# Role adapters: first projections by eight samples of one role, on two Strassen levels, with the weights stationary

## The chip, the core and the metric

The kernel runs on one core of one Trainium2 chip. Its time is device microseconds from launch to end, the median of several runs on the chip. One execution is also recorded by the hardware profiler; its trace gives the durations used here. PE is the matrix engine (PEld its weight loads), DVE the vector engine, ACT the scalar engine, POOL GpSimd, SP the engine whose queue issues nearly all DMAs. SBUF is the on-chip memory of 128 partitions, PSUM the matrix engine's accumulators in banks of 512 f32 columns, DRAM the chip's main memory.

## What is computed

128 samples, each a 128 x 1024 f32 matrix, go through two layers. In each layer a sample uses the weights of its own role, which is in an input list; there are three sets of weights.

```python
for W_down, b_down, W_up, b_up, gamma, beta in layers:     # two layers
    h = gelu(x @ W_down[role] + b_down[role])              # 1024 -> 512, per sample
    y = x + h @ W_up[role] + b_up[role]                    # 512 -> 1024
    x = layernorm(y) * gamma[role] + beta[role]
```

All of it is in f32.

## The kernel before

**Order of the samples.** A short sort on the chip, mostly on DVE, counts the roles and puts the samples into slots, so that slots 2n and 2n+1 hold two samples of one role: 63 such pairs, and a last item of two samples whose roles may differ. `perm` gives the sample of a slot, `place` its role's place; both are read into registers (`reg`).

**Four phases.** Layer 0 down, layer 0 up, layer 1 down, layer 1 up, each over 64 items. A down item reads two samples (`quartered`, L399: four DMAs of 128 KB each per sample), transposes them on DVE (`turn`, L557), multiplies by `W_down`, applies the Gelu and stores the hidden states to a DRAM buffer `hd`. An up item reads `hd`, transposes it (L668 to L671), multiplies by `W_up`, adds the sample, normalises and stores the result to a DRAM buffer `mid` or to the output.

**Strassen on a pair.** The two samples of a pair are the two row blocks of the left matrix; its columns are halved, and the weights are cut into four blocks. Winograd's form of Strassen's method needs seven products of blocks where the plain way needs eight. The left sums (`winograd_sums`, L413) are four operations on POOL. The right sums, T1 to T4, are made once for each role (`Sums`, L173): loaded into the room of the tables, summed on DVE, stored to DRAM (`scratch`), and loaded from there for the phase. SBUF holds the seven blocks of all three roles (`wall`), and a product picks its role by a register in the address. In `product` (L423) the samples are the stationary operand and the weights the moving one, 256 columns in a down phase, 512 in an up phase:

```python
nc.tensor.matmul(ps[:, 0:cols], a[:, j], w.rhs(r, j, cols), ...)
```

The products of an item accumulate in PSUM banks of three groups, `b` (3 banks), `e` (3) and `a` (2). ACT first copies the bias into a bank (`seeded`). Between products DVE or ACT copies partial results out of a bank (`begin`, `end`, `whole`; called evictions here), and a later product adds to the same bank. The last item has the two samples alone, four products each.

**Order of the work.** `at(time, step)` puts a step into a heap; at the end the steps are issued in order of time, and each engine executes its instructions in that order. The unit is one product of a pair, four matmuls of 256 columns or two of 512; an item takes seven units, and its seven products stand two units apart, so that two items' products alternate on PE. `Down.PREPARE`, `Up.PREPARE` and the loop at L865 set how far ahead loads, transposes and sums stand. All DMAs of this loop stand in SP's queue, in the same order of time, and wait there for the buffers that they fill or read.

The first item of layer 0 is different (`plain`, L589): its two samples belong to the commonest role and are multiplied without Strassen, since their weights have only just arrived.

Of the kernel before, what the change touches and what calls it, by code (L numbers as in the profile page):

```python
# [11 lines left out]
I32 = mybir.dt.int32  # L12
AF = mybir.ActivationFunctionType
# [6 lines left out]
P = 128  # L20
# [6 lines left out]
def kernel(  # L27
# [11 lines left out]

# [4 lines left out]
    NPAIR = (B - R + 1) // 2  # L61
    NFIRST = -(-B // R) // 2
    W = H
    ORDER = ["B11", "B21", "T2", "T1", "T3", "B22", "T4"]

    const = ctx.enter_context(tc.tile_pool(name="const", bufs=1))
    wpool = ctx.enter_context(tc.tile_pool(name="weights", bufs=1))
    work = ctx.enter_context(tc.tile_pool(name="work", bufs=2))
# [3 lines left out]

    NI = NPAIR + 1
    hd = [dram.tile([2, S * K], F32, tag=f"hd{n}", name=f"hd{n}") for n in range(NI)]
    mid = [dram.tile([2, S, H], F32, tag=f"mid{n}", name=f"mid{n}") for n in range(NI)]
    scratch = {
        (layer, up): {
            t: dram.tile([P, R, W], F32, tag=f"{t}_{layer}{up}", name=f"{t}_{layer}{up}")
            for t in ORDER
        }  # L80
        for layer in range(2)
        for up in (0, 1)
    }

    def flat(tag, bufs, name, size=2048):
        return work.tile([P, size], F32, tag=tag, name=name, bufs=bufs)


    NSLOT = 8
    wall = wpool.tile([P, NSLOT, R * W], F32, name="wall")  # L90

    class Block:


        def __init__(self, slot):
            self.slot = slot
            self.v = wall[:, slot].rearrange("p (r n) -> p r n", n=W)

        def rhs(self, r, j, cols):
            return self.v[:, ds(r, 1), ts(j, cols)]  # L100

    class Half:


        def __init__(self, v, half):
            self.v, self.half = v, half

        def rhs(self, r, j, cols):
            return self.v[:, ds(r, 1), j, self.half]

    tables = wpool.tile([P, 3, R * H], F32, name="tables")

    def table(v, which):
        n = v.shape[1]
        t = tables[:, which].rearrange("p (r n) -> p r n", r=R)[:, :, 0:n]

        def load(places=range(R), queue=nc.sync):
            for k in places:  # L120
                r = reg(role_of, k, [queue.engine], R - 1)
                queue.dma_start(t[:, k], v[ds(r, 1), :].to_broadcast((P, n)))

        return t, load

    def bias_table(v, which):

        n = v.shape[1] // 2
        t, load = table(v, which)

        def subtract(places=slice(0, R)):
            right, left = t[:, places, n:], t[:, places, 0:n]
            nc.vector.tensor_tensor(right, right, left, ALU.subtract)

        return t, load, subtract


    rows_of = [
        wall[:, 2 * k : 2 * k + 2]
        .rearrange("p k n -> p (k n)")  # L140
        .rearrange("p (r j h c) -> p r j h c", r=R, h=2, c=K // 2)
        for k in range(2)
    ]

    def load_rows(k, place, queue):
        role = reg(role_of, place, [queue.engine], R - 1) if place else reg(role_0, 0, [queue.engine], R - 1)
        src = layers[0][0][ds(role, 1)].rearrange("o (p m) c -> p (o m) c", p=P)
        queue.dma_start(rows_of[k][:, place].rearrange("p j h c -> p j (h c)"), src[:, ts(k, NQ)])

    first_weights = {  # L150
        "B11": Half(rows_of[0], 0),
        "B21": Half(rows_of[1], 0),
        "B22": Half(rows_of[1], 1),
        "T3": Half(rows_of[0], 1),
        "T1": Block(4),
        "T2": Block(5),
        "T4": Block(6),
    }

    def first_sum(name, place):  # L160
        b11, b12, b21, b22 = (rows_of[k][:, :, :, h] for k in range(2) for h in range(2))
        t1, t2, t4 = (
            first_weights[n].v.rearrange("p r (j c) -> p r j c", c=K // 2) for n in ("T1", "T2", "T4")
        )
        o, a, b = {
            "T1": (t1, b12, b11),
            "T2": (t2, b22, t1),
            "T3": (b12, b22, b12),
            "T4": (t4, b21, t2),
        }[name]  # L170
        nc.vector.tensor_tensor(o[:, place], a[:, place], b[:, place], ALU.subtract)

    class Sums:  # L173

        def __init__(self, layer, up, k):
            self.w = layers[layer][2 if up else 0]
            self.rows = "o (m i) c -> i (o m) c" if up else "o (i m) c -> i (o m) c"
            self.k = k  # L180
            n = self.w.shape[2] // 2
            room = tables[:, 0:2].rearrange("p t n -> p (t n)")
            self.whole = room[:, 0 : 4 * W].rearrange("p (m c) -> p m c", c=2 * n)
            block = lambda t: t.rearrange("p (j c) -> p j c", c=n)
            quarter = room[:, 0 : 4 * W].rearrange("p (k j h c) -> p k h j c", k=2, h=2, c=n)
            self.at = {
                "B11": quarter[:, 0, 0],
                "B12": quarter[:, 0, 1],
                "B21": quarter[:, 1, 0],
                "B22": quarter[:, 1, 1],  # L190
                "T1": block(room[:, 4 * W : 5 * W]),
                "T2": block(room[:, 5 * W : 6 * W]),
            }
            self.at["T3"], self.at["T4"] = self.at["B12"], self.at["B21"]
            self.to = {name: block(t[:, k]) for name, t in scratch[layer, up].items()}

        def load(self, q):
            if q == 0:
                self.role = reg(role_of, self.k, [ENG.SP], R - 1)
            rows = self.w.shape[1] // NQ  # L200
            src = self.w[ds(self.role, 1), ds(q * rows, rows), :]
            nc.sync.dma_start(self.whole[ts(q, SQ)], src.rearrange(self.rows, i=SQ))

        def sum(self, name):
            a, b = {"T1": ("B12", "B11"), "T2": ("B22", "T1"), "T3": ("B22", "B12"), "T4": ("B21", "T2")}[name]
            nc.vector.tensor_tensor(self.at[name], self.at[a], self.at[b], ALU.subtract)

        def store(self, name):
            nc.sync.dma_start(self.to[name], self.at[name])

    class Phase:
        def __init__(self, layer, up):
            self.layer, self.up, self.weights = layer, up, {}
            self.vectors = layers[layer][3:] if up else layers[layer][1:2]
            if up:
                self.gamma, self.load_gamma = table(self.vectors[1], 1)
                self.beta, self.load_beta = table(self.vectors[2], 2)

        def new_bias(self, which):
            self.next_bias, self.load_bias, self.subtract = bias_table(self.vectors[0], which)  # L220

# [827 lines left out]
```

## Time and profile before

| what | us |
|---|---|
| median of 3 runs (3123.8 to 3123.97) | 3123.83 |
| profiled execution | 3123.5 span, nothing outside it counted |
| PE busy | 3111.5 |
| DVE, POOL, ACT busy | 1975.9, 1770.7, 1200.7 |
| DVE busy in 200 us of a down phase of layer 0 / of an up phase | 100.0 / 155.7 |
| POOL busy in the same | 91.5 / 140.6 |
| products of the first item end | 31.9 |
| last product of an up item in layer 1 begins | 3110.9 |

The profile has one line for a group of instructions: source line, engine, operation, the tile written and the tiles read, shapes and count; then the busy time and the mean duration of one; then the time that the engine was idle just before them and what ended it. Matmuls are pipelined, so that the durations of neighbours overlap; their true spacing is read from the chain or from starts. The chain of waits follows the work that ended last back to the start. A matmul of f32 operands appears as two instructions.

### The profile page before, as it was taken

To read this page: it belongs to the slowest core of one execution; us is meant where nothing else is said; L and a number is where in the kernel's file an instruction comes from. 1 tells how busy PE (TensorE), PEld (TensorE's weight loads), DVE (VectorE), ACT (ScalarE), POOL (GpSimd) and SP (SyncE) were. 2 spreads that over 40 slices of the span, in tenths; PEclk is the share of its full clock that TensorE was granted. 3 is DMA by queue.
4 is the path that set the end of the run, shared out by engine and by line. 5 is a ranking of instruction groups with operands and counts; after the bars stand their busy time and mean duration, and the time that the engine had idled before them with its cause. 6 is when DMAs were issued, how large, how long until landed. Compare 5 with 4: busy or idle time off the path is not lost.

```text
span 3123.5 us, 42240 instructions
## 1 busy us (share of the span) xinstructions
PE 3111.5 (100%) x10796; PEld 2048.3 (66%) x10796; DVE 1975.9 (63%) x2814; ACT 1200.7 (38%) x2813; POOL 1770.7 (57%) x1388
## 2 busy tenths in 40 slices
PE   9999999999999999999999999999999999999999
PEld 6888888888544444444488888888884444444443
DVE  6554544544678777777864444444447877777777
ACT  1222222222454545555432222222224545554544
POOL 3544344444577767777654443434436777677775
PEclk9999999999999999999999999999999999999999
DMA  8778788886786565666687555555567765656564
GB/s 218 197 216 209 209 207 210 213 209 194 272 293 236 215 223 215 218 220 217 230 237 182 144 128 135 126 130 134 128 189 272 282 235 210 226 204 230 208 230 174
DMA packets 429880, 642.22 MB, mean 206 GB/s; under 512 B 35794, under 2 KB 305875, under 8 KB 428500
## 3 DMA queue, kind: packets, MB, share of 16 engines
q1 hardware_dynamic: 429074, 637.15, 66.4%
q8 instruction: 102, 1.67, 0.2%
q10 hardware_dynamic: 578, 2.36, 0.2%
q14 instruction: 126, 1.03, 0.1%
HBM read 405.02 MB, written 234.36 MB: 205 GB/s over the span
## 4 chain that ended last, share of the span: by engine, by line
PE 50%; DVE 0%; issue 0%; ACT 0%; DVEq 0%
PE bu L427 14%; PE bd L427 14%; PE eu L427 7%; PE ed L427 7%; PE au L427 4%; PE ad L427 3%; DVE ou L725 0%; DVE last_stat L701 0%; DVE xu L700 0%; ACT ou L809 0%; DVEq L1045 0%; DVE xu L694 0%; DVE last_mv L719 0%; DVEq L365 0%; ACT meanu L807 0%
## 5 line engine op out<-in xcount | busy, mean ns | idle before, releaser
L427 PE MATMUL bu<-wall,hTu 128*128 (+1 forms) x2048 | 921.4, 592 | 0.4 <-DVE xu L694 0.4
L558 DVE STREAM_TRANSPOSE xTd<-xqd 128x1024 f32<-128x1024 f32 (+1 forms) x252 | 504.5, 2065 | 348.5 <-PE bd L427 280.8
L427 PEld LDWEIGHTS bu<-wall,hTu 128*128 128x128 f32 x2048 | 389.0, 190 | 488.1 <-issue 454.4
L418 POOL TENSOR_TENSOR Sd<-xTd 128x512 f32<-128x512 f32 x123 | 158.5, 1289 | 791.1 <-DVE xTd L558 787.6
L811 POOL TENSOR_TENSOR varu<-varu,mhalf 128x1 f32<-128x1 f32 x254 | 327.2, 1288 | 394.6 <-ACT varu L810 394.6
L427 PE MATMUL eu<-wall,hTu 128*128 (+1 forms) x1040 | 488.0, 592 | 0.0
L427 PE MATMUL bd<-wall,xTd 128*128 (+1 forms) x2048 | 483.1, 379 | 0.0
L427 PE MATMUL bd<-wall,Sd 128*128 (+1 forms) x2000 | 472.5, 379 | 0.0
L427 PEld LDWEIGHTS bd<-wall,xTd 128*128 128x128 f32 x2048 | 389.1, 190 | 54.2 <-issue 1.4
L427 PEld LDWEIGHTS bd<-wall,Sd 128*128 128x128 f32 x2000 | 380.0, 190 | 52.9 <-issue 1.4
L818 DVE SCALAR_TENSOR_TENSOR ou<-xu,meanu,tables 128x1024 f32<-128x1024 f32 x253 | 325.9, 1288 | 134.3 <-ACT ou L809 120.1
L624 ACT ACTIVATE hd<-hd 128x256 f32<-128x256 f32 x379 | 157.8, 417 | 531.3 <-DVE hd L623 531.3
L427 PEld LDWEIGHTS eu<-wall,hTu 128*128 128x128 f32 x1040 | 197.6, 190 | 247.5 <-issue 219.1
L805 ACT ACTIVATE partu<-statu 128x2 f32<-128x2 f32 x254 | 51.6, 203 | 729.6 <-DVE xu L703 729.6
L809 ACT ACTIVATE ou<-xu,meanu 128x1024 f32<-128x1024 f32 x254 | 291.7, 1148 | 8.6
L826 POOL TENSOR_TENSOR ou<-ou,tables 128x1024 f32<-128x1024 f32 x123 | 290.1, 2359 | 0.0
L694 DVE TENSOR_TENSOR xu<-bu,xu 128x512 f32<-128x512 f32 x256 | 176.0, 687 | 118.3 <-PE bu L427 118.3
L427 PE MATMUL ed<-wall,xTd 128*128 (+1 forms) x1056 | 249.1, 379 | 0.0
L418 POOL TENSOR_TENSOR hTu<-hTu 128x256 f32<-128x256 f32 x126 | 198.1, 1573 | 70.7 <-DVE hTu L669 47.5
L427 PE MATMUL au<-wall,hTu 128*128 (+1 forms) x504 | 236.8, 592 | 0.0
L427 PE MATMUL ed<-wall,Sd 128*128 (+1 forms) x1000 | 236.2, 379 | 0.0
L427 PE MATMUL ad<-wall,xTd 128*128 (+1 forms) x992 | 234.3, 379 | 0.0
(146 smaller groups left out, 3395.8 us busy)
## 6 DMA issues: line engine op xcount, KB each, us to landing
xqd<-in_x_dram SPq DMA_DIRECT2D x512, 128.0 KB, 3.2
hd<-hd SPq DMA_DIRECT2D x256, 256.0 KB, 2.4
xu<-in_x_dram SPq DMA_DIRECT2D x128, 512.0 KB, 3.8
mid<-ou SPq DMA_DIRECT2D x128, 512.0 KB, 4.4
xu<-mid SPq DMA_DIRECT2D x128, 512.0 KB, 3.8
out_dram<-ou SPq DMA_DIRECT2D x125, 512.0 KB, 3.7
hqu<-hd SPq DMA_DIRECT2D x244, 256.0 KB, 5.0
xqd<-mid SPq DMA_DIRECT2D x488, 128.0 KB, 3.8
```

The lines of the kernel that those rows point to most:

```text
L418: engine.tensor_tensor(dst[:, 1], a11, a21, ALU.subtract)
L427: nc.tensor.matmul(ps[:, 0:cols], a[:, j], w.rhs(r, j, cols), start=start and j == 0, stop=j == n - 1, skip_group_check=True,)
L558: nc.vector.transpose(self.a[:, s, chunks].rearrange("p j (t a) -> p j a t", t=SQ), self.xq[s].rearrange("p a (i j) -> p j a i", i=SQ)[:, ...
L624: nc.scalar.activation(y, y, AF.Gelu)
L694: nc.vector.tensor_tensor(y, ps, y, ALU.add)
L805: nc.scalar.mul(part, self.stat[:, s], -1.0 / H)
L809: nc.scalar.activation(box["o"], self.x[:, s], AF.Square, bias=m, accum_out=v)
L811: nc.gpsimd.tensor_tensor(v, v, mhalf[:, 0:1], ALU.pow)
L818: nc.vector.scalar_tensor_tensor(box["o"], self.x[:, s], box["m"][:, 0:1], row(self.ph.gamma), ALU.add, ALU.mult)
L826: nc.gpsimd.tensor_tensor(o, o, row(self.ph.beta), ALU.add)
```

## The change

The down phases are rewritten; the up phases keep their products and get other inputs.

- **Octets.** Slots 2 to 113 form 14 octets, eight samples of one role each. Four samples side by side make one row block of 512 columns in the transposed layout. An octet has the seven outer products of the Strassen-Winograd form; six of them (`INNER`) are themselves done by the same method on a second level, with seven inner products of two matmuls each; T3 (`PLAIN`) is done whole with eight matmuls.
- **Weights stationary.** In the down phases the weights are the stationary operand and the transposed samples the moving one: 256 columns (two samples) for inner products, 512 for T3. The hidden states come out transposed and are stored so; the up items load them without a transpose.
- **Left sums.** The outer sums of an octet (s3, A21, s2, s4, each in two halves) are on DVE, the second half of s4 on POOL. The inner sums (d1, d3, d0, d2 of six outer products) are on POOL.
- **The rest.** Slots 0 and 1 and six pairs (slots 114 to 125) are multiplied plainly, 32 matmuls of 256 columns a pair, with unsummed weights; slots 126 and 127 singly, 32 matmuls of 128 columns each. Pairs 0 and 57 come first in a layer, the other five and the two singles between octets 8 and 9.
- **Weights by role.** SBUF holds one role's down weights (all blocks of both levels) and one role's up weights. `DownJob` and `UpJob` make the sums of the other roles on DVE and store them to DRAM, during layer 0's octets (two down roles, then three up roles), layer 0's up phase (three down roles for layer 1) and layer 1's octets (three up roles). Where two neighbouring items may differ in role, every block's load stands in SP's queue with a flag (`cond`), a register computed by comparing the roles: the DMA moves data only if the flag is set. Bias, gamma and beta of the up items are single-role tables in two sets, loaded in the same way.
- **The sort** is longer: it forms octets, pairs and singles, and computes the flags.

The diff, cut to its core:

```diff
-    NPAIR = (B - R + 1) // 2
+    NOCT = 14
+    SURE = 5
+    NLEFT = 6
     ORDER = ["B11", "B21", "T2", "T1", "T3", "B22", "T4"]
+    INNER = ["B11", "B21", "T2", "T1", "B22", "T4"]
+    PLAIN = [q for q in ORDER if q not in INNER]
...
-    wall = wpool.tile([P, NSLOT, R * W], F32, name="wall")
+    down_w = region("down_w", NU * UNIT)
+    up_w = region("up_w", 10 * 1024)
+    blocks = region("blocks", 7 * 2048)
+    units = region("units", 8 * 512)
+    results = region("results", 3 * 2048)
+    staged = region("staged", 3 * 1024)
...
+    class DownWeights:
+        def load(self, layer, q, role, cond=None):
+            kw = {} if cond is None else {"cond": cond, "cond_hint": False}
+            src = down_scratch[layer][q][ds(role, 1)].rearrange("o p n -> p (o n)")
+            nc.sync.dma_start(self.whole[q], src, **kw)
...
+    class DownJob:
+        def steps(self, start, pace):
+            s = [(start + 0.6 * q, lambda q=q: self.load(q)) for q in range(NQ)]
+            t = start + 5
+            for name in ("T1", "T2", "T3", "T4"):
+                s.append((t, lambda name=name: self.sum(name)))
+                t += 2.2 * pace
+            for k, q in enumerate(INNER):
+                ops = inner_sums(self.at[q], self.extra[k % 4])
+                for op in ops:
+                    s.append((t, op))
+                    t += 0.5 * pace
+                s.append((t + 0.4, lambda q=q, k=k: self.store(q, k % 4)))
...
+    class Turns:
+        def turn(self, s, k, to, at_col):
+            waiting[self.k[s]] -= 1
+            v = self.xq[s].rearrange("p a (j i) -> p j a i", i=SQ)
+            nc.vector.transpose(
+                to[:, :, at_col : at_col + P].rearrange("p j (a t) -> p j a t", t=SQ), v[:, ts(k, 4)]
+            )
...
+    class PlainItem:
+        def chunk(self, j):
+            for f in range(4):
+                nc.tensor.matmul(
+                    self.ps[f][:, 0 : self.n],
+                    raws[self.parity][:, j, ts(f, P)],
+                    self.v[:, j, 0 : self.n],
...
+    class Octet:
+        def multiply(self, ps, q, w, v, start, stop):
+            for j, u in enumerate(dw.unit(q, w)):
+                nc.tensor.matmul(
+                    ps[:, 0:256], u, v[:, j], start=start and j == 0, stop=stop and j == 1, skip_group_check=True
+                )
...
+        def carry(self, q):
+            ps = self.ps[q]
+            ps["x"] = bank("a", self.tag + q)
+            nc.scalar.copy(ps["x"][:, 0:256], ps["b"][:, 0:256])
...
+        def steps(self, base, turns=True):
+            put = lambda t, f: e.append((base + 0.5 * t, f))
...
+            for t, name in ((-1.4, "s3"), (1.4, "A21"), (4.2, "s2"), (8, "s4")):
+                for half in range(2):
+                    engine = nc.gpsimd if name == "s4" and half else nc.vector
+                    put(t + 1.5 * half, lambda n=name, h=half, g=engine: self.outer(n, h, g))
...
+                for k, name in enumerate(("d1", "d3", "d0", "d2")):
+                    put(b - 5.6 + 1.6 * k, lambda q=q, n=name: self.inner(q, n, nc.gpsimd))
+                for k, p in enumerate(PS):
+                    put(b + 2 * k, lambda q=q, p=p: self.product(q, p))
+                put(b + 1, lambda q=q: self.carry(q))
+                for t, args in (
+                    (3, ("e", 1, 1, True, False)),
+                    (5, ("b", 0, 1, True, False)),
+                    (7, ("x", 0, 0, True, True)),
+                    (9, ("b", 1, 1, False, True)),
+                    (11, ("e", 0, 1, False, True)),
+                    (13, ("b", 1, 0, True, True)),
+                ):
+                    put(b + t + 0.1, lambda q=q, args=args: self.flow(q, *args))
...
     class Up:
...
-            for s in range(2):
-                nc.vector.transpose(
-                    self.a[:, s].rearrange("p j (a t) -> p j a t", t=SQ),
-                    self.hq[s].rearrange("p a (j i) -> p j a i", i=SQ),
-                )
...
+        def seeded(self, t):
+            ps = bank(t, self.tag)
+            if self.m < 3:
+                cleared(ps)
+            nc.scalar.copy(ps, self.t["bias"][:, ts("be".index(t), K)])
```

An octet's steps are given in half-steps, half of the old unit: two matmuls of 256 columns. Its seven outer products begin at half-steps 0, 7, 14, 21, 28, 36 and 43, and the next octet at 50. The inner products of one outer product stand two half-steps apart, so that those of two neighbours alternate on PE. `flow` is the eviction of one inner result, by ACT where it only copies and by DVE where it adds.

## The prediction

> **What bounds the kernel now.** I read four views. First the page's busy times and slices, to see whether one engine bounds all of it:
>
> ```profile
> span 3123.5 us, 42240 instructions
> PE 3111.5 (100%) x10796; PEld 2048.3 (66%) x10796; DVE 1975.9 (63%) x2814; ACT 1200.7 (38%) x2813; POOL 1770.7 (57%) x1388
> PE   9999999999999999999999999999999999999999
> PEld 6888888888544444444488888888884444444443
> ```
>
> PE is full in every slice. PEld tells the four phases apart: 8 is a down phase (256-column products), 4 an up phase (512-column ones). Second, the table by stretches, a down one and an up one of layer 0:
>
> ```profile
> 200.00:400.00 200.00, 200.00 (x928) 176.06 (x927) 100.00 (x95) 55.02 (x151) 91.46 (x63) 1.00 0.78 211
> 1000.00:1200.00 200.00, 200.00 (x467) 88.54 (x466) 155.70 (x264) 100.86 (x216) 140.63 (x113) 1.00 0.61 220
> ```
>
> After the span the columns are PE, PEld, DVE, ACT, POOL, clock, DMA share, GB/s. In the down phase DVE and POOL are only half busy, so a change that takes PE work away and gives them work has room there on average. Third, the chain, whose pieces give the true spacing of matmuls (the groups' means, 379 and 592 ns, overlap):
>
> ```profile
> 1549.52 3.43 PE bu L427 x8
> 1573.60 3.45 PE bd L427 x16
> ```
>
> One instruction takes 428.8 ns at 512 columns (3.43/8) and 215.8 ns at 256 (3.45/16; 16 products of 8 from 31.89 to 59.51 us give the same). Each matmul of the program is two such instructions: 28 matmuls x 2 x 62 pairs of layer 0, 63 of layer 1, and twice 64 for the two single samples make the 7128 records of the down phases. Fourth, the groups, for the price of one of everything:
>
> ```profile
> L558 DVE STREAM_TRANSPOSE xTd<-xqd 128x1024 f32<-128x1024 f32 x248 | 500.2, 2080 | 344.9 <-PE bd L427 280.8 <-POOL Sd L421 36.0 <-DMA hd<-hd 9.2
> L669 DVE STREAM_TRANSPOSE hTu<-hqu 128x512 f32<-128x512 f32 x256 | 166.5, 689 | 0.0
> L623 DVE TENSOR_TENSOR hd<-ed,hd 128x256 f32<-128x256 f32 x129 | 54.6, 423 | 156.2 <-PE ed L427 156.2
> L206 DVE TENSOR_TENSOR tables<-tables 128x1024 f32<-128x1024 f32 x36 | 46.5, 1293 | 0.0
> L418 POOL TENSOR_TENSOR Sd<-xTd 128x512 f32<-128x512 f32 x123 | 158.5, 1289 | 791.1 <-DVE xTd L558 787.6
> L427 PEld LDWEIGHTS bd<-wall,xTd 128*128 128x128 f32 x2048 | 389.1, 190 | 54.2 <-issue 1.4
> ```
>
> **PE's work, part by part.** *Octets.* An octet of eight samples has seven outer products. Six are split again: 6 x 7 x 2 = 84 matmuls of 256 columns; T3 stays whole: 8 of 512. That is 168 x 0.2158 + 16 x 0.4288 = 43.1 us. Four pairs cost 4 x 56 x 0.2158 = 48.3 us now. Saved 5.2 us, 28 times (14 octets, two layers): -146.
>
> *Plain pairs.* They lose their one Strassen level: 64 instructions for 56, +1.73 us each; 6 in layer 0 and 7 in layer 1 (layer 0's first pair is plain already): +22.
>
> *Singles.* Each of the two is 64 instructions of 128 columns. No row has that shape. The lower end is half of 215.8 ns, 108 ns; the upper is a load followed by its product without overlap, 190 + 108 = 298 ns. The nearest row is the load itself: loads run beside products now, and 190 ns is longer than 108. I take 190: 2 x 64 x 0.190 = 24.3 us per layer against 13.8, +21 in both; ends 0 and +49.
>
> [...] This trace's f32 loads take 190. [...]
>
> *Up products* are the same 3592. The twelve clearing matmuls of the first three up items (the opening's bf16 zeros: eight in 2.43 us) add 3. *Start:* the sort gets some 30 more small DVE operations, at about 0.15 us (fifteen take 2.15 us from 6.9 to 9.06 us now), and the first transposes wait for it; the first item now ends at 31.9 us, I put it at 34: +2 (0 to 5, since the weights' 2 MB must land too).
>
> PE's sum: -146 + 22 + 21 + 3 + 2 = -98.
>
> **DVE and POOL beside it.** Per octet DVE has 16 transposes. They now write contiguously, as L669's do, so I take 0.69 us, not half of 2.08. With them come seven outer sums of 128x1024 (L206's row; 1.22 where POOL is quiet), 28 evictions (0.42), T1's four sums (0.38) and T3's four operations (0.69): 36 us of 43. POOL has 24 sums of 128x512 (1.27 us and 0.08 between) and half of s4 (2.36, L826's row): 35 of 43. Each alone is covered by PE. But they do not run alone. This is the timeline of the move from up to down, DVE against POOL:
>
> ```profile
> 1557.08 1.27 POOL L419 TENSOR_TENSOR wall<-wall 128x512 f32<-128x512 f32 x1
> 1557.70 1.73 DVE L828 SCALAR_TENSOR_TENSOR ou<-ou,varu,tables 128x1024 f32<-128x1024 f32 x1
> 1558.43 2.13 POOL L420 TENSOR_TENSOR Sd<-wall 128x512 f32<-128x512 f32 x1
> 1559.36 0.68 DVE L694 TENSOR_TENSOR xu<-bu,xu 128x512 f32<-128x512 f32 x1
> 1559.96 1.69 DVE L818 SCALAR_TENSOR_TENSOR ou<-xu,meanu,tables 128x1024 f32<-128x1024 f32 x1
> 1560.64 2.13 POOL L421 TENSOR_TENSOR Sd<-wall,Sd 128x512 f32<-128x512 f32 x1
> ```
>
> A DVE operation with both inputs in SBUF and a POOL sum take turns: DVE's L828 starts 0.65 us before POOL ends and is 0.5 us longer than its usual 1.25; L420 waits for it in turn. L694, with one input in PSUM, is not touched. So the outer sums wait for the inner ones.
>
> *Where it hurts.* The outer sums stand around an octet's first product, from 1.2 us before it. A half-step (two matmuls) is 0.863 us. DVE must do seven outer sums (1.15 back to back) and six evictions (0.35) before the one that B11's seventh product waits for: 8.05 + 2.1 = 10.2 us, ending 9.0 us after the octet's start. That product is due at 12 half-steps, 10.4 us. If no sum waits, there is no stall. If all seven wait a whole POOL sum (1.1 us) the eviction comes at 16.7 and PE stalls 6.3 us. In between, POOL has about five sums to do in that stretch (B21's four and T2's first), each costing DVE the rest of one, 0.5 to 0.85: it ends at 11.5 to 13.2 us. I take 2.0 us of stall per octet; ACT's copy of B21's bank, queued behind a Gelu that waits for the same evictions, gives nearly the same delay and does not add to it. 28 x 2.0 = +56, ends 0 and +176.
>
> *Weight sums.* Two of layer 0's roles need 4 + 24 two-input sums each, 12 us of DVE and about 10 of waits over 76 us; 11.9/76 of this falls in each tight stretch, 3.4 us in 3.5 octets. The six sets of up weights are four large sums each (7.6 us with waits, over 46.6): 1.9 us in 6.6 octets. Together 25; half lies behind the last deadline: +13, ends 0 and 25.
>
> *What costs nothing.* The transposes gone from the up phases (256 x 0.61 us) lie beside a full PE. ACT's 26 or so short operations per octet (0.37 to 0.42) fill 12 of 43 us. SP issues 32 loads per octet at 0.5 us and 8 register loads at 0.35, 19 us. Transfers are 6 MB per octet, 140 GB/s against 211 now. A sample's load goes out once the transposes three samples back are done and lands in 3.7 us; its turn comes some 7 us later. If that cover is gone, the transposes and all evictions behind them are late. In an up pair, SP gets ten flagged loads (0 to 0.43 us each: no row shows a skipped one) and three register loads, 5.3 us on top of about 3 in 12. They wait for PE or DVE and hold the next hidden-state load behind them, which has 20 us in hand. Where the flag is set, 512 KB lands in 5 us, a whole item ahead.
>
> **Sum.** -98 + 56 + 13 = -29. The profiled execution took 3123.5 us; the median of the runs is 3123.83, 0.3 above, so the forecast is 3095.
>
> **Rivals.**
> 1. *The turns are harmless.* The 36 and 35 us of 43 speak for it; then -98, 3026, and with up to 1 us per octet 3055.
> 2. *DVE is the bound, and it is slower.* The mechanism is the same taking of turns at the octets' starts. For it: DVE's 36 us plus thirteen waits of 0.35 are 41 of 43, so a lag once made is hardly won back. Against it: the back-to-back rate (0.61 for 0.69) gives 4 us back. It decides from (98 - 13)/28 = 3.0 us of stall per octet; at 5 us the time is 3123.8 - 98 + 140 + 25 = 3191.
> 3. *Singles load without overlap:* 298 ns, +28 more: 3123, no change. Against it: loads lie wholly beside products in every row now.
>
> **How the numbers follow.** The forecast case (1 to 3 us per octet) gets 0.45, rival 1 0.20, rival 2 0.30, rival 3 0.05. Its own range is 3067 to 3123. About 0.2% (6 us) is what a measurement of this kernel tells from no change: of the forecast case 0.06 lies there, of rival 2 0.01, of rival 3 0.02; 0.61 faster, 0.09 same, 0.30 slower. The range 3035 to 3175 leaves out the better part of rival 1's best third (0.08) and rival 2 above 4.5 us per octet (0.12).
>
> **What would show it.** PE's spacing still 0.216 us inside an octet, with one gap of about 2 us at each octet's start, released by a DVE eviction or an ACT copy; POOL sums of 2.1 us in that stretch; longer gaps in the first four octets of layer 0; singles of 12 us; up phases as long as now (768 us of products). Wrong would be: gaps spread over the whole octet (DVE as the bound), PE waiting for transposes or their loads, SP late with flagged loads in an up phase.

## The result and the profile after

The changed kernel takes 3298.38 us (median of 4 runs, 3292.68 to 3304.57) beside 3123.9 for the kernel before on the same chip: 1.0558 times as long, 95% interval 1.0543 to 1.0573. The forecast was 3095 with a range up to 3175, so the direction was wrong and the time lies outside the range. The profiled execution has a span of 3302.7 us. First the page's busy times and slices:

```profile
span 3302.7 us, 41272 instructions
PE 3076.3 (93%) x9944; PEld 1876.2 (57%) x9944; DVE 2468.1 (75%) x3795; ACT 1152.6 (35%) x2573; POOL 2168.8 (66%) x1593
PE   6879989899999898999978899999999999999998
PEclk8989999999999999999989999999999999999999
```

PE is no longer full. A slice is 82.6 us; the first three are thin, and the sixth, the eighth (578 to 661 us), the 14th and 16th (1073 to 1156 and 1239 to 1321) and the 21st to 23rd (1652 to 1899). The clock is down in the first, third and 21st. By the first products, the four phases (down, up, down, up) take 857.5, 852.5, 796.4 and 796.2 us; before they took 789.9, 771.5, 775.2 and 786.9. The up phase of layer 0, whose products were not changed, lost most. The table by stretches (PE, PEld, DVE, ACT, POOL, clock, DMA share, GB/s) compares the first octets, one quiet octet and the stretch of the up phase shown of before:

```profile
60.00:260.00 200.00, 155.68 (x603) 119.28 (x602) 174.79 (x261) 39.31 (x98) 122.71 (x82) 0.92 0.57 178
719.37:765.32 45.95, 44.11 (x185) 34.67 (x184) 38.30 (x60) 11.84 (x29) 37.34 (x25) 1.00 0.43 138
1000.00:1200.00 200.00, 184.59 (x417) 79.02 (x416) 157.39 (x240) 92.96 (x197) 128.74 (x102) 0.98 0.71 238
```

A quiet octet takes 46.0 us, 2.9 over its 43.1 of products. The first four of layer 0 take 56.7, 60.6, 62.0 and 51.7. In the up phase PE ran 417 products in 200 us instead of 467.

In the quiet octet the timeline of DVE, POOL and PE shows the mechanism of the prediction, at 2.9 us where it gave 2.0:

```profile
718.18 2.10 DVE L639 TENSOR_TENSOR blocks<-blocks 128x1024 f32<-128x1024 f32 x1
720.87 3.42 DVE L639 TENSOR_TENSOR blocks<-blocks 128x1024 f32<-128x1024 f32 x2
723.29 2.13 POOL L657 TENSOR_TENSOR units<-units,blocks 128x512 f32<-128x512 f32 x1
724.55 1.95 DVE L639 TENSOR_TENSOR blocks<-blocks 128x1024 f32<-128x1024 f32 x1
725.50 2.13 POOL L660 TENSOR_TENSOR units<-blocks,units 128x512 f32<-128x512 f32 x1
724.69 1.13 PE L666 MATMUL bo_10T<-blocks,down_w 128*128 128x256 f32 x4 [0.84 <-DVE results L715]
731.40 1.10 PE L666 MATMUL bo_11B<-units,down_w 128*128 128x256 f32 x4 [0.85 <-ACT ao_11B L691]
```

The outer sums (L639) take up to 2.1 us, POOL's sums 2.13 instead of 1.27, and PE stops twice: at 724 a product of T4 of the octet before waits for an eviction of DVE, and at 731 B21's third product waits for ACT's copy of B21's bank (`o…B` stands for B11, B21 and B22 alike). Each stop is 1.01 us of lost spacing; the other 0.8 us lies in small pieces just behind them.

What the forecast did not have is elsewhere. Gaps of PE in the first octets are released by evictions that DVE does late. In the up phase they are released by DVE and, where the role changes, by the weights' loads:

```profile
1186.75 2.35 POOL L1056 TENSOR_TENSOR units<-units,results 128x1024 f32<-128x1024 f32 x1
1186.89 2.49 DVE L352 TENSOR_TENSOR down_w<-down_w 128x256 f32<-128x256 f32 x1
...
1662.65 1.88 PE L830 MATMUL eu<-up_w,blocks 128*128 128x512 f32 x4
1669.86 5.93 PE L830 MATMUL bu<-up_w,blocks 128*128 128x512 f32 x8 [5.33 <-DMA up_w<-u0B]
1685.74 1.95 PE L830 MATMUL bu<-up_w,blocks 128*128 128x512 f32 x4 [1.27 <-DMA up_w<-u0B]
1697.77 3.22 PE L830 MATMUL eu<-up_w,blocks 128*128 128x512 f32 x4 [4.88 <-DMA up_w<-u0B]
```

The first pair of lines is a sum of a weight job, 0.38 us where POOL is quiet (L352 at 48.39 us), that takes 2.49 us because it waits for a POOL operation of 2.35. In the others up products wait for blocks of up weights, up to 5.3 us at a time.

### The profile page after: what moved, and what is told of

It is laid out like the page before. It is cut to its first block, busy times and chain, and to the rows that moved or that the text cites. A ratio compares the mean times of both kernels' runs of the same rounds, so it can differ in the third digit from the quotient of the medians.

```text
span 3302.7 us, 41272 instructions
## 1 busy us (share of the span) xinstructions
PE 3076.3 (93%) x9944; PEld 1876.2 (57%) x9944; DVE 2468.1 (75%) x3795; ACT 1152.6 (35%) x2573; POOL 2168.8 (66%) x1593
## 5 line engine op out<-in xcount | busy, mean ns | idle before, releaser
L830 PE MATMUL bu<-up_w,blocks 128*128 128x512 f32 x2016 | 918.3, 597 | 35.1 <-DVE blocks L944 14.1
L830 PEld LDWEIGHTS bu<-up_w,blocks 128*128 128x128 f32 x2016 | 382.4, 191 | 527.7 <-issue 459.1
L830 PE MATMUL eu<-up_w,blocks 128*128 128x512 f32 x1008 | 481.1, 600 | 16.1 <-DMA up_w<-u0B 9.0
L541 DVE STREAM_TRANSPOSE blocks<-staged 128x512 f32<-128x512 f32 x512 | 338.3, 688 | 174.1 <-DMA staged<-in_x_dram 92.2
L651 POOL TENSOR_TENSOR units<-blocks 128x512 f32<-128x512 f32 x168 | 248.4, 1479 | 319.2 <-DVE blocks L541 240.3
L697 ACT ACTIVATE results<-results,bcolo 128x256 f32<-128x256 f32 x392 | 210.2, 538 | 662.8 <-DVE results L715 432.0
L1035 ACT ACTIVATE partu<-statu 128x2 f32<-128x2 f32 x254 | 51.7, 203 | 821.7 <-DVE blocks L944 815.4
L639 DVE TENSOR_TENSOR blocks<-blocks 128x1024 f32<-128x1024 f32 x196 | 329.6, 1708 | 0.0
L1039 ACT ACTIVATE units<-blocks,meanu 128x1024 f32<-128x1024 f32 x250 | 287.1, 1148 | 8.6
L660 POOL TENSOR_TENSOR units<-blocks,units 128x512 f32<-128x512 f32 x168 | 242.4, 1443 | 13.2
L830 PE MATMUL au<-up_w,blocks 128*128 128x512 f32 x504 | 240.8, 601 | 7.3 <-DMA up_w<-u0B 4.4
L654 POOL TENSOR_TENSOR blocks<-blocks 128x512 f32<-128x512 f32 x112 | 154.9, 1383 | 7.8 <-DVE blocks L639 1.2
L657 POOL TENSOR_TENSOR units<-blocks 128x512 f32<-128x512 f32 x112 | 150.3, 1342 | 8.6
```

The lines of the kernel that those rows point to most:

```text
L541: nc.vector.transpose(to[:, :, at_col : at_col + P].rearrange("p j (a t) -> p j a t", t=SQ), v[:, ts(k, 4)])
L639: engine.tensor_tensor(o, a, b, op)
L651: engine.tensor_tensor(d["d1"], m(0, 0), m(1, 0), sub)
L657: engine.tensor_tensor(d["d0"], d["d3"], m(0, 0), sub)
L660: engine.tensor_tensor(d["d2"], m(0, 1), d["d0"], sub)
L697: nc.scalar.activation(y, y, AF.Gelu, bias=self.bias[:, f : f + 1])
```

## The experiments

Each kernel was run beside the kernel before, which took 3124 to 3125 us every time, so that the medians compare. "Octets" are times from the first product of one to that of the next.

### Four causes, one at a time

**Outer sums with one input.**

```diff
-            engine.tensor_tensor(o, a, b, op)
+            if engine is nc.vector:
+                nc.vector.transpose(o, b)
+            else:
+                engine.tensor_tensor(o, a, b, op)
```

> The outer sums of the octets that DVE makes (seven per octet) become one-input transposes of the same tile, so the hidden states are not those of the reference; the half of s4 on POOL stays a sum, and nothing moves. Theory: the octet's stall comes from DVE operations with two SBUF inputs taking turns with POOL's sums. A transpose takes about as long by itself (0.69 us for 512 columns, so 1.38 for 1024, against 1.21 for the sum with POOL quiet), but in the trace transposes do not get longer beside POOL. Then an undisturbed octet goes from 46.0 to 43.1 to 43.7 us and the whole from 3298 to 3220 to 3240. Rival, that DVE is simply full at the start of an octet: the transposes occupy it no less, octets stay at 45.5 or more and the time at 3285 or more.

Measured: 3230.63 us, 67.8 less. The group of these operations in the changed kernel, then in this one (busy us and mean ns, then idle time before), and this kernel's table for a quiet octet:

```profile
L639 DVE TENSOR_TENSOR blocks<-blocks 128x1024 f32<-128x1024 f32 x196 | 329.6, 1708 | 0.0
```

```profile
L640 DVE STREAM_TRANSPOSE blocks<-blocks 128x1024 f32<-128x1024 f32 x196 | 233.5, 1217 | 0.0
```

```profile
694.27:737.40 43.13, 43.13 (x185) 34.96 (x184) 33.80 (x61) 11.84 (x29) 33.45 (x25) 1.00 0.46 147
```

A transpose of the tile takes 1217 ns, as the sum does beside a quiet POOL (1.21), so the operations themselves are as long as before; only the waiting is gone, 491 ns of each. The quiet octet takes 43.13 us, exactly its products. The stall of a quiet octet is the taking of turns, and nothing else.

**No weight jobs in layer 0's octets.**

```diff
-            for k in (1, 2):
-                job = DownJob(0, up_w, lambda e, k=k: reg(role_0, k, e, R - 1), None)
...
+            t += 84
```

> The two DownJobs of layer 0 and the flagged reloads of layer 0's down weights are left out, so that all octets of layer 0 use the commonest role's weights. Theory: octets 0 to 3 of layer 0 (56.7, 60.7, 62.0, 51.6 us) are long because of these jobs; without them each takes 46 to 47 us, 42 to 47 us less in all, 3252 to 3257. Rival, that the octets after the start are late for another reason (samples' loads behind the start's, the sort): they stay above 52 us each, and the time above 3275.

Measured: 3261.74 us, 36.6 less, 5 above the theory's range. Octets 0 to 3: 53.0, 46.0, 46.0, 46.0. The reloads that are left out too stand in octets 4 and later, so in octets 1 to 3 the jobs are the cause; octet 0 keeps 7 us for another reason (below).

**No weight jobs in layer 0's up phase.**

```diff
-            for r in range(R):
-                steps, t = DownJob(1, down_w, lambda e, r=r: r, None).steps(t, 4)
...
-                at(T - 45 + 5 * k, lambda q=q: dw.load(1, q, top_role(ENG.SP)))
```

> The three DownJobs of layer 1, the loads of their sums and layer 1's flagged reloads of down weights are left out, so that layer 1's octets use the weights still in SBUF from layer 0. Theory: in the up phase of layer 0 (852.5 us) the jobs' sums on DVE and their waits for loads cost about 45 us between 880 and 1410 us; the phase becomes 805 to 812 and the whole 3250 to 3258. Rival, that they fit beside PE there and the loss is the flagged loads': phase 840 or more, 3285 or more.

Measured: 3245.86 us, 52.5 less; the phase is 791.7 us instead of 852.5. In the stretch shown above PE is full again with 457 products:

```profile
1000.00:1200.00 200.00, 197.57 (x457) 87.08 (x456) 149.18 (x227) 99.70 (x211) 141.65 (x114) 0.99 0.62 212
```

**No flagged loads in the up phases.**

```diff
-                at(
-                    max(when + 1.2, prev + 0.95),
-                    lambda box=box, name=name, c=c, layer=layer: load_wu(layer, name, box["r"], box[c]),
-                )
...
-                    lambda box=box, which=which, layer=layer, m=m: load_table(layer, m % 2, which, box["r"], box["c2"]),
```

> All flagged loads of up weights and of bias, gamma and beta (item 21 on, both layers) are left out, so that these items use the commonest role's. Theory: only the loads that really move data cost, where the role changes: the gaps of PE at 1310 to 1314 and 1619 to 1750 us that a load of up weights ends, or that lie between such gaps, sum to 36 us in the up phase of layer 0, and 9 in that of layer 1; so 3298 becomes 3250 to 3262. Rival 1, that skipped loads also hold SP and with it the hidden states in all items from the 21st on: gaps of quiet items (1320 to 1600) go too, 3235 or less. Rival 2, that DVE and POOL are late there and the loads only end last: 3280 or more.

Measured: 3255.84 us, 42.5 less: 30.2 in the up phase of layer 0, 10.4 in that of layer 1. The theory's range holds; the loads that move data cost, not the skipped ones: from 500 to 700 us into layer 0's up phase PE is busy for 197 us with the flagged loads and without.

### All four together

> All four edits of the first runs together: DVE's outer sums as one-input transposes, no DownJobs in either layer, no flagged reloads of down weights, no flagged loads of up weights and tables (the UpJobs stay). It computes the products of the change with one role's weights. If the four causes are separate, their differences add: 3298.4 - 67.8 - 36.7 - 52.5 - 42.6 = 3099. If they share gaps or the slow clock after them, it ends above that, 3110 to 3130; if one hides another, below, 3070 to 3090. What is left above the 3026 that PE's sum without any stall gives must be the start, the octets behind the plain pairs and the UpJobs.

Measured: 3083.73 us, 1.3% under the kernel before (ratio 0.987, 0.9853 to 0.9886). The four differences sum to 199.5; together they are worth 214.6. So they are nearly separate, and partly make each other worse. Even with all of this work left out, it is 58 us over the 3026 that the forecast's PE sum gives. The trace places them: first octet 15.2 later than forecast (63.0 for 47.8); octet 0, 7.8 long; octets behind the plain pairs 7.7 and 7.1; octets beside the UpJobs 9.1 and 13.5; the start of layer 1, 11.1 over two pairs; the five pairs and two singles 2.7 each layer over their products; less 20 for the singles, which were priced too high. That is 57.

### What makes the weight jobs dear

**One-input sums.** All `DownJob` and `UpJob` sums become transposes of the same tiles (`inner_sums` likewise):

```diff
-            tt(self.at[name], self.at[a], self.at[b], sub)
+            nc.vector.transpose(self.at[name], self.at[b])
```

> All sums of the DownJobs and UpJobs become one-input transposes of the same tiles at the same places, so the weights of all roles but the commonest are not those of the reference. By the first runs the DownJobs cost 43.5 us in octets 0 to 3 of layer 0 and 60.8 us in its up phase. Theory 1, taking turns with POOL: the 4 large and 24 small sums of a job are as long as alone (1.3 and 0.4 us) and most of that goes: octets 0 to 3 lose no more than 4 to 5 us each, the up phase is 800 to 815 us, the octets beside UpJobs 46 to 47; the whole 3205 to 3225. Theory 2, DVE waits in order: the first sum of a job stands at its load, which the sums' kind doesn't change: the gaps of 10.4 and 6.5 us in octets 0 and 2 and of 7.4 us at 1260 stay, and the whole is 3255 to 3275.

Measured: 3252.58 us, 45.8 less, below the range of theory 2 and far above that of theory 1. Octets 0 to 3 take 53.7, 57.5, 54.3, 51.6 (13.9 less in all), the up phase 831.2 (21.3 less), the octets beside UpJobs in layer 1 47.0 (3.5 less each). Taking turns is about a third of the jobs' price in layer 0.

**A longer lead.**

```diff
-            t = start + 5
+            t = start + 13
             for name in ("T1", "T2", "T3", "T4"):
```

> A DownJob's first sum is issued 13 units after its loads instead of 5 (13.8 us later); nothing else is changed, and the output is that of the reference. Theory 2 (DVE waits in order for the load): the large gaps go, 10.4, 6.5 and 6.8 us in octets 0 to 2 and 4.6, 7.4 in the up phase of layer 0: octets 0 to 3 come to 50 to 53 us, 16 to 24 less in all, the up phase is 10 to 20 us shorter, the whole 3255 to 3272. Theory 1 (turns with POOL): the sums cost the same a little later, the whole stays at 3285 or more.

Measured: 3285.92 us, 12.5 less, by the time just on theory 1's side. By stages both hold in part: the up phase gets 14.9 shorter, as theory 2 has it. In the octets the wait moved: octet 2 goes from 62.0 to 47.4, octet 3 from 51.7 to 58.1, octets 0 and 1 stay at 56.7 and 60.6. So the gap of 10.4 us in octet 0 was not the job's load; I had laid it there wrongly.

**Transfers without sums.**

```diff
         def sum(self, name):
+            if self.skip:
+                return
...
-                    s.append((t, op))
+                    if not self.skip:
+                        s.append((t, op))
```

> The DownJobs of layer 1 keep all their loads and stores, and only their sums on DVE are left out (layer 1's weights are then not the reference's). Without the jobs the up phase of layer 0 took 791.7 us instead of 852.5; with one-input operations in place of the sums 831.2. Theory: DVE's time is what the jobs cost; without the sums the phase comes to 790 to 797 us, the whole to 3236 to 3246. Rival, that the transfers of the jobs (24 MB read and written beside the up phase's own) cost: the phase stays at 815 or more, the whole at 3260 or more.

Measured: 3254.57 us; the up phase is 803.4 us, between the two theories and nearer the first. Of the 61 us that the jobs cost there, 12 are their transfers (with the loads of layer 1's first down weights), 49 DVE's sums; of these 21 are the turns, and 15 could be had by a longer lead. The last two may overlap.

### Moving the outer sums

**Earlier.**

```diff
-                    t = -28 + 3.3 * s
+                    t = -28 + 3.3 * s if s < 4 else -15.2 + 2.7 * (s - 4)
...
-            for t, name in ((-1.4, "s3"), (1.4, "A21"), (4.2, "s2"), (8, "s4")):
+            for t, name in ((-5.6, "s3"), (-2.6, "A21"), (0.4, "s2"), (10, "s4")):
```

> The transposes of an octet's samples 4 to 7 stand 2.7 half-steps apart instead of 3.3, and the outer sums begin at half-steps -5.6 (s3), -2.6 (A21), 0.4 (s2) and 10 (s4) instead of -1.4, 1.4, 4.2 and 8; the output is that of the reference. Theory: DVE's sums still take turns with POOL's, but most of them are done before the first evictions of the octet are due; a quiet octet goes from 46.0 to 43.5 to 44.5 us, 28 times 1.5 to 2.5: 3228 to 3256. Rival, that the lag is DVE's and only moves: the evictions of the octet before then wait behind the sums, and octets stay at 45.5 to 47, 3285 to 3330.

Measured: 3411.78 us, 113 more, further out than even the rival had it. Quiet octets take 51.2 us. PE's timeline where one octet goes over into the next:

```profile
707.57 1.13 PE L666 MATMUL bo_9T<-units,down_w 128*128 128x256 f32 x4 [1.56 <-DVE results L715]
713.74 1.13 PE L666 MATMUL bo_9T<-blocks,down_w 128*128 128x256 f32 x4 [2.15 <-DVE results L715]
716.07 1.91 PE L666 MATMUL bo_10B<-blocks,down_w 128*128 128x256 f32 x4
```

Both long waits now lie in T4 of the octet before (`bo_9T`), whose evictions stand behind the sums in DVE's order, and after them the products run at half their rate for some 3 us (1.91 us for four instead of 1.03). DVE is busy for 39.7 of 51.3 us here: it is not full; what stands in front of an eviction in its order decides.

**One outer sum later.**

```diff
-                    t = -28 + 3.3 * s
+                    t = -25 + 2.9 * s
...
-            for t, name in ((-1.4, "s3"), (1.4, "A21"), (4.2, "s2"), (8, "s4")):
+            for t, name in ((-1.4, "s3"), (1.4, "A21"), (4.2, "s2"), (21, "s4")):
-                    engine = nc.gpsimd if name == "s4" and half else nc.vector
+                    engine = nc.vector
...
-                put(b + 13.6, lambda q=q: self.give(self.LEFT[q]))
+                put(b + (17.5 if q == "B21" else 13.6), lambda q=q: self.give(self.LEFT[q]))
```

> s4's two halves are moved from half-steps 8 and 9.5 (the second on POOL) to 21 and 22.5, both on DVE, where POOL has no sums because T3 needs none; A12's block is kept until then, and the next octet's transposes begin three half-steps later at 2.9 apart; the output is that of the reference. Theory: turns at the octet's start are the cause, and three sums fewer there (two of DVE, one of POOL of 3.3 us) take away most of the stall: a quiet octet goes from 46.0 to 43.3 to 44.5 us, the octets behind the pairs (52.9) to 48 to 50; the whole 3225 to 3262. Rival, as in the kernel with earlier outer sums: DVE is simply full and the lag turns up elsewhere, octets of 45.5 to 48, 3285 or more.

Against what the expectation says of its output, s4 is formed here after T2's inner sum d3 has changed s2 in its place, so its values are not those of the reference; the operations are the same in number and size. Measured: 3332.5 us, 34 more. Quiet octets take 47.3 us, with gaps of 1.46, 1.00 and 1.03 us. The first is new: a product of B22 waits for ACT's copy of B22's bank (first row; the second row is a gap kept from before):

```profile
720.39 1.10 PE L666 MATMUL bo_10B<-units,down_w 128*128 128x256 f32 x4 [1.32 <-ACT ao_10B L691]
734.41 1.13 PE L666 MATMUL bo_10T<-blocks,down_w 128*128 128x256 f32 x4 [0.84 <-DVE results L715]
```

```profile
751.38 2.17 DVE L639 TENSOR_TENSOR blocks<-blocks 128x1024 f32<-128x1024 f32 x1
753.70 1.28 POOL L654 TENSOR_TENSOR blocks<-blocks 128x512 f32<-128x512 f32 x1 [1.23 <-DVE blocks L639]
```

POOL's stretch was not quiet: its sums for B22 wait for s4 itself (L654 waits 1.23 us for L639), and the transposes, pushed together, now stand between T3's evictions, behind which ACT's copy comes late. The rival is right that the lag turns up elsewhere; its reason, a DVE full by its own work, is refuted by the one-input sums. So neither of the two places tried is free for these sums while POOL works beside them; others were not tried.

**The same with the lead and earlier loads of layer 1's first weights.**

```diff
-            t = start + 5
+            t = start + 13
...
-                at(T - 45 + 5 * k, lambda q=q: dw.load(1, q, top_role(ENG.SP)))
+                at(T - 105 + 5 * k, lambda q=q: dw.load(1, q, top_role(ENG.SP)))
```

> The previous kernel with the DownJobs' first sum at 13 units after the loads instead of 5, and the loads of layer 1's first down weights 60 units earlier; the output is that of the reference. The lead alone gave 12 us. If the gains add: 12 us under the previous kernel by the lead and 5 to 15 by the loads, which then do not meet the role changes at the end of the up phase; the last 60 us of that phase get shorter by as much. Otherwise within 5 us of the previous kernel.

Measured: 3300.57 us, 31.9 less than the kernel with the later s4, more than the two were given. (Its s4 has the same wrong values.) The up phase of layer 0 went from 854.9 to 828.4.

**Everything mended.** The earlier outer sums, these two edits, and UpJobs of layer 1 at a pace of 4:

> The outer sums of the previous kernel, the lead of 13 units in the DownJobs, the loads of layer 1's first down weights 60 units earlier (so that they don't meet the role changes at the end of the up phase), and UpJobs of layer 1 at a pace of 4 instead of 1.6; the output is that of the reference. If the four causes add: 3298 less 42 to 70 (outer sums), 26 to 43 (lead), 10 to 15 (loads at the role changes), 5 (UpJobs): 3165 to 3215, still above the 3124 of before. If the waits replace each other, 3230 or more.

Measured: 3387.86 us, 24 less than the earlier outer sums alone (3411.78). The mends of the jobs keep their worth; the outer sums' move undoes it.

### The octet behind the plain pairs

**Weight loads on another queue** (with the lead and the earlier loads above):

```diff
-                            item.r = reg(role_at, slot, [ENG.SP], R - 1)
-                        c = reg(left_changed, idx, [ENG.SP], 1) if idx >= 3 else None
-                        load_raw(layer, item.parity, item.r, [nc.sync], parts=1 if only is None else 4, cond=c, only=only)
+                        on, queue = (ENG.Activation, nc.scalar) if idx >= 3 else (ENG.SP, nc.sync)
...
+                        load_raw(layer, item.parity, item.r, [queue], parts=1 if only is None else 4, cond=c, only=only)
```

> The kernel after the change with three edits, and the reference's output: the DownJobs' lead of 13 units, layer 1's first down weights loaded 60 units earlier, and the flagged loads of the plain items' weights (from the fourth on) moved from SP's queue to ACT's. The first two gave 32 us together beside the later s4. Theory for the third: octet 9's samples come late because their loads stand in SP's queue behind weight loads that wait for PE (12.6 us between 560 and 626); on ACT's queue they wait for nothing else, the gap of 8.9 us at 637 and of 8.4 at 2287 in layer 1 go, and octet 9 takes 46 to 48 us instead of 52 to 53: 12 less over both layers. The whole: 3298 - 32 - 12 = 3254. Rival, that the ring of three samples and the landing of their loads set the pace: octet 9 stays at 51 to 53, the whole at 3266.

Measured: 3289.03 us (3275.54 to 3293.02), above both sides of the expectation. Octet 9 takes 50.7 and 49.9 us, 2 less, and the pairs ahead of it 6 to 7 more; the gap of 8.7 us stays. The waits in SP's queue between 560 and 626 us, of the changed kernel and of this one:

```profile
SPq L316 <- PE ep L580: 12.6, 2, 7.9
```

```profile
SPq L534 <- DMA up_w<-in_L_cond_W_down_dram: 28.1, 6, 9.3
```

The samples' loads (L534) now wait on SP for the weights' transfers themselves. Why they should, from another queue, the code doesn't say, and it was not settled.

**No weight loads for these items.**

```diff
-                    if alone and layer:
+                    if idx >= 3:
+                        pass
+                    elif alone and layer:
```

> The flagged loads of the plain items' weights are left out from the fourth item on (items 60 to 62 and the two singles, both layers), so that these items use the weights already in SBUF. Theory: octet 9's samples come late because their loads share the time and the queue with these weight loads; then the gap of 8.9 us in octet 9 of layer 0 and of 8.4 in layer 1 shrink to under 2, octet 9 takes 46 to 47.5 us instead of 51.7 to 52.9, and the five pairs with two singles 130 to 131 with octet 8 instead of 132 to 133: 3298 becomes 3280 to 3285. Rival, that three rooms for samples in flight set the pace by themselves: octet 9 stays at 50 or more, the time above 3290.

Measured: 3293.56 us. Octet 9 takes 47.7 and 48.3 us instead of 52.9 and 51.7: the weight loads are 5.2 of the 6.9 us that it loses in layer 0, and 3.4 of 5.7 in layer 1. In layer 0 a gap of 5.4 us, released by the same eviction, is left, and SP's longest wait in that stretch is now this one:

```profile
SPq L597 <- ACT bcolp L551: 30.0, 4, 8.3
```

The stores of the plain items' hidden states (L597) wait for the items to be finished, with octet 9's samples behind them. So neither side of the expectation holds as put: it is SP's order that makes the samples late, by two kinds of waiting DMA, of which only one was taken away; the second is read from the queue and was not tested. The rooms for samples weren't varied, but the loads' own waits for a free room (L534 for the transposes, L541) sum to 0.3 us in this stretch of the changed kernel.

## Why the prediction was wrong

Of the 203 us between forecast and result the terms are as follows.

*PE's sum, octets.* Right: 43.1 us an octet, and 43.13 where nothing waits.

*Singles, +21.* Wrong, +1. A product of 128 columns follows the next at 0.11 us:

```profile
606.40 0.39 PE L580 MATMUL ep<-blocks,up_w 128*128 128x128 f32 x2
606.62 0.39 PE L580 MATMUL bp<-blocks,up_w 128*128 128x128 f32 x2
```

Two in 0.22 us, so the load's recorded 190 ns is how long one takes, not how far apart they can be. How close two loads can come at the least the rows don't show: 108 ns, half of 215.8, is what the product itself takes, by my estimate. This error was in the kernel's favour: 20 us.

*Start, +2.* Wrong, +15. The first product of octet 0 comes at 61.8 us; 34 and a plain pair of 13.8 make 47.8. PE's first plain product begins at 25.0 us instead of 15.1, and the second pair waits 5 us more for its samples. Then octet 0 has a gap of 10.4 us that I had not priced at all: its transposes are late, so the seven outer sums stand together in front of the first evictions. DVE's timeline shows two reasons:

```profile
45.42 1.30 DVE L541 STREAM_TRANSPOSE blocks<-staged 128x512 f32<-128x512 f32 x2 [10.36 <-DMA staged<-in_x_dram]
54.67 1.48 DVE L352 TENSOR_TENSOR down_w<-down_w 128x256 f32<-128x256 f32 x1
70.70 9.06 DVE L639 TENSOR_TENSOR blocks<-blocks 128x1024 f32<-128x1024 f32 x7
```

DVE waits 10.4 us for samples, and then the commonest role's own 24 inner sums (L352 to L355) stand between octet 0's transposes: 15.8 us from 48.4 to 69.6, in which DVE is hardly ever idle. The forecast priced these sums for the two other roles alone. The kernels without DownJobs keep the gap (10.7 us, 8.6 with all four out), so it is not theirs; how it divides between loads and sums is open, since no kernel leaves either out.

*Stall of 2.0 us an octet, +56.* The mechanism was right, with both releasers and POOL's 2.1 us: 2.9 us in a quiet octet, 67.8 us for the whole by the one-input sums. The place was not: the sum was made for B11's seventh product, which loses only 0.2 us. A third of the stall lies in T4 of the octet before, and another third at ACT's copy of B21's bank, behind a Gelu as foreseen, which was to add nothing. That 2.0 came so near to 2.9 is partly luck. It is 12 us of the miss.

*Weight sums, +13.* The step that failed first. "Half lies behind the last deadline" assumed that an octet has slack for the other half. It has little that such sums can use: DVE is 38.3 us busy in 46.0 and in order. The two DownJobs' sums occupy DVE for 52 us in octets 0 to 3, and 36.6 us of it appear in the time. The UpJobs add 24, by the length of the octets beside them (48.1 to 52.0 for 46.0; no kernel leaves them out): 61 for 13.

*The up phases.* The second failure is an omission: layer 1's three DownJobs run in layer 0's up phase, and the sum had no term for them, though the forecast's own table shows DVE at 155.7 and POOL at 140.6 of 200 us there. They cost 52.5 us: 84 sums in the phase where both engines were busiest.

*Flagged loads, 0.* "512 KB lands in 5 us, a whole item ahead" looked at one block. At a change seven blocks and three tables replace each other, each free only after the item before has used it, beside the phase's own transfers. PE waits up to 5.3 us for one. 42.5 us in both layers. The skipped ones are as cheap as the forecast took them: 0.07 to 0.09 us each on SP.

*Plain pairs.* Their products cost what was said; the octets behind them lose 12.6 us and layer 1's first pairs 11 to 20, on loads that stand late in SP's queue. The forecast named loads held in SP's queue for the up phases only.

Without the 20 for singles these are 15 + 12 + 48 + 52 + 43 + 13 + 7 (octet 0) and, for layer 1's start, some 11 that the flagged loads don't cover: 201 - 20 = 181. Some 22 of 203 are left, not much more than the 15 that the four causes gain by being together.

Rival 2 had the right direction by the wrong reason: it decides at 3.0 us a quiet octet, and the octets stayed at 2.9. Of the signs named beforehand for a wrong forecast, gaps spread over a whole octet did not come. The others did: octet 9's transposes wait for late loads, and in the up phases PE waits for flagged loads.

## What to carry to other kernels

Price a two-input sum on DVE by the engine beside it: next to a POOL that is two thirds busy (66% of the span), each of 1.2 us cost 0.5 more, and what counted was not DVE's share but which eviction stood behind it in order. List every stage that an edit gives work to before summing, also those whose products don't change; the largest term of the miss was work moved into a phase that I had counted as untouched. A weight that is replaced in place by a flag costs next to nothing when skipped (here 0.08 us of its queue), but at a change its whole set must pass between two items, so sum the set, not one block.

## What the runs showed of the hardware

The gaps cost more than their length. Around the gap of octet 0 (PE stops at 69.8 us and resumes at 80.15), the changed kernel's table by stretches and PE's timeline read:

```profile
69.80:75.00 5.20, 0.00 (x0) 0.00 (x0) 5.20 (x6) 0.00 (x0) 0.00 (x0) 0.86 1.07 219
75.00:80.00 5.00, 0.00 (x0) 0.00 (x0) 5.00 (x5) 0.00 (x0) 3.44 (x2) 0.50 1.06 228
80.00:85.00 5.00, 4.85 (x14) 4.00 (x15) 3.70 (x6) 0.88 (x3) 4.92 (x3) 0.62 0.44 105
85.00:90.00 5.00, 5.00 (x25) 4.41 (x24) 3.27 (x6) 1.42 (x5) 4.84 (x4) 1.00 0.02 5
```

```profile
80.15 2.07 PE L666 MATMUL bo_0B<-blocks,down_w 128*128 128x256 f32 x4 [10.42 <-DVE results L709]
82.02 1.91 PE L666 MATMUL ao_0B<-blocks,down_w 128*128 128x256 f32 x4
84.63 1.03 PE L666 MATMUL bo_0B<-units,down_w 128*128 128x256 f32 x4
```

The granted clock (last column but two) has a mean of 0.86 from 69.8 to 75 us and of 0.50 from 75 to 80, while PE does nothing. In the 5 us from 80 on, in which PE is busy for 4.85, it is 0.62, and four instructions take 2.07 and 1.91 us; from 85 us on it is 1.00, and four take 1.03. By these figures the products behind the gap cost 1.8 us more than at a clock of 1.00 (an estimate, 0.38 of 4.85). Behind a shorter wait the clock is lowered too. In the kernel with earlier outer sums the table around the wait of 2.15 us, which ends at 713.74, reads:

```profile
709.00:711.30 2.30, 2.25 (x11) 1.60 (x9) 2.30 (x3) 1.32 (x4) 2.22 (x2) 1.00 0.41 171
711.30:713.70 2.40, 0.28 (x2) 0.00 (x0) 2.40 (x3) 0.00 (x0) 2.32 (x2) 1.00 0.67 273
713.70:715.00 1.30, 1.26 (x6) 1.14 (x7) 0.41 (x2) 1.28 (x4) 0.78 (x1) 1.00 0.00 0
715.00:717.00 2.00, 2.00 (x7) 1.56 (x6) 0.33 (x1) 1.03 (x3) 0.00 (x0) 0.51 0.11 36
717.00:719.00 2.00, 2.00 (x8) 1.65 (x7) 0.00 (x0) 0.36 (x1) 0.00 (x0) 0.64 0.89 283
```

PE is busy for 0.28 of the 2.40 us from 711.3 to 713.7, and the clock is still 1.00 there and up to 715; from 715 to 717 it is 0.51 and from 717 to 719 it is 0.64, though PE is busy throughout.

Summed over the time in which PE is busy, the share of the clock that was not granted comes to 46.9 us in the changed kernel (mean granted clock over the span 0.980), 1.7 in the one before (0.999) and 17.6 with all four causes out (0.991). So some 45 of the 203 us are the clock's; they lie inside the terms above. The four kernels with one cause out (0.980, 0.983, 0.984 and 0.981) lose 2.7, 7.7, 10.2 and 1.5 us less by it, 22 together, the one with all out 29: that is 7 of the 15 us by which the four causes are worth more together than singly.
